# A GRU with an expert-choice layer behind it: state products by halves of the columns, VectorE's order in a step, and the order of the loads at the start

## The chip, the core and the metric

The kernel runs on one core of a Trainium2 chip. The metric is the time of one execution on the device in microseconds (us), of which the median of several runs is given. Beside the runs there is one profiled execution, from which all views of the trace come. TensorE is the matmul engine; each of its matmuls is preceded by a load of its stationary operand, shown as PEld. VectorE (DVE) and ScalarE (ACT) do the elementwise work, GpSimd (POOL) small copies, and SyncE (SP) issues most transfers.

## The reference

The input x has 16 sequences of 256 steps with 512 features. A GRU runs over the steps; its state h is 16 x 512, from `cond` at the start.

```python
gi = x @ W_ih + b_ih            # 512 -> 3 x 512
gh = h @ W_hh + b_hh
r = sigmoid(i_r + h_r)
z = sigmoid(i_z + h_z)
n = tanh(i_n + r * h_n)
h = (1 - z) * n + z * h
```

All 256 states form a 4096 x 512 matrix `xf`. A router computes `softmax(xf @ router_w + router_b)` over 16 experts; each expert takes its 256 tokens of highest weight. All experts share one matrix, so the output is x plus, for each token, the sum of the weights with which it was taken, times `xf @ expert_w + expert_b`. Everything is float32.

## The kernel before

**Layout.** A state product has only 16 rows. It is therefore laid out by four column tiles of the array: of the 512 columns of a gate, tile j computes every fourth group of 32, and its 128 columns land in partitions 32j and following of a PSUM bank (`quadrant`, `columns`). The contraction over 512 features is in four parts k. So one gate of one step is 4 k x 4 j = 16 matmul calls of 128 columns. In float32 each call becomes two loads and two matmuls in the trace. Two steps, an even and an odd one, form a pair p and share a bank half; the odd step multiplies both steps' states (32 columns of the stationary operand) so that its result lands beside the even one's.

**A step** (the loop over `s`). TensorE computes r and n over k = 0, 1, then r and n over k = 2, 3, then all of z (`h_part`, L424). The preset of these banks, by ScalarE copies, already holds x's contribution for r and z (from `ring`) and the bias for n (`preset_first` L384, `preset_rest` L387 and L394). ScalarE applies the sigmoid to r (L503). VectorE copies one element of r into `seen` (L507), multiplies r with h's part of n (L551), adds x's part (L553), each by halves of the columns. ScalarE applies tanh to the two halves (L555) and one sigmoid to all of z (L556). VectorE transposes both by 32 x 32 blocks (`turn_n` L563, `turn_z` L566), and computes u = h - n (L569), v = u z (L574) and the new state v + n (L577), each half by itself. The first half of the new state holds k = 0, 1, the second k = 2, 3.

While this chain runs, TensorE does other work in the same step: half of x's product for a pair six pairs ahead (`x_part` L401; `x_done` L412 adds the bias and stores it in `ring`), and, from the 13th step on, units of the expert product of finished groups (`expert` L368, one unit is a quarter of the columns for one k, four calls). Eight steps form a group g; a group's x is transposed into `xT` (two buffers, `turn_x` L234). The last expert products run after the steps (`late_part` L114), together with the search for each expert's threshold.

**The order** of all engines' work around the change is written out by hand (`manual_schedule`): each engine executes its instructions in the order of the program text, and semaphores are set between them where they touch the same data.

**The head**, before the first step. Six banks are zeroed and two spare banks zeroed repeatedly, each by four matmuls with a zero operand of 32 columns (`begin_sums`, `keep_clock`, L89). The input weights `wih` come gate by gate, each in two halves on SyncE's and ScalarE's queues, first r, then n, then z, with x's first group (SyncE) and `cond` (ScalarE) behind the first gate; `whh` follows by gates. x's second group comes on GpSimd's queue. TensorE transposes x's first group (`spread_x` L454, with VectorE copies L457), computes gate after gate for the first four pairs (`x_gate`), transposes `cond` and x's second group in between, adds the biases (`biases` L272), and completes the fifth pair. The sixth pair's product (index `AHEAD - 1` = 5) is spread over the odd steps of the first eight and stored at step 7.

Of the kernel before, what the change touches and what calls it, by code (L numbers as in the profile page):

```python
# [17 lines left out]
def kernel(  # L18
# [43 lines left out]
    zero = const.tile([P, QD], BF16, name="zero")  # L62
    nc.gpsimd.memset(zero, 0.0)
    make_identity(nc, ident)

# [19 lines left out]
    def begin_sums(bank):  # L85

        n = bank.shape[-1]
        for j in range(KC):
            nc.tensor.matmul(  # L89
                bank[QD * j : QD * (j + 1)],  # L90
                zero,
                zero[:, 0:E].unsqueeze(1).to_broadcast([P, n // E, E]),
                start=True,
                stop=True,
                tile_position=(0, QD * j),
            )

    early_groups = list(range(15))

# [64 lines left out]
    with (  # L164
# [78 lines left out]
        with tc.manual_schedule(engines={ET.SP, ET.Activation, ET.Pool}):  # L243
            def load_gate(dst, src, form, i, gate):
                load_rows(dst[:, :, i, :], src[:, gate * D : (gate + 1) * D], form)

            load_gate(wih, w_ih, "(p c) n -> p c n", 0, 0)
            nc.sync.dma_start(out=xs[:, 0, :], in_=x[:, 0:TG, :])
            nc.scalar.dma_start(out=c0, in_=cond)
            load_gate(wih, w_ih, "(p c) n -> p c n", 1, 2)  # L250
            load_gate(wih, w_ih, "(p c) n -> p c n", 2, 1)
            for gate in (0, 2, 1):
                load_gate(whh, w_hh, "(c p) n -> p c n", gate, gate)
            nc.scalar.activation(dummy, ones[0:1, 0:1], AF.Sigmoid)
            for dst, src in (
                (b_raw[0:1], b_ih.rearrange("(o g d) -> o g d", o=1, d=D)),
                (b_raw[1:2], b_hh.rearrange("(o g d) -> o g d", o=1, d=D)),
                (b_n, b_hh[2 * D :].rearrange("(o d) -> o d", o=1)),
            ):
                nc.gpsimd.dma_start(out=dst, in_=src)  # L260
            nc.gpsimd.dma_start(out=xs[:, 1, :], in_=x[:, TG : 2 * TG, :])
            for j in range(KC):
                load_xa(2, xa2, j, (nc.sync, nc.sync))
            nc.sync.dma_start(out=ewr[:, :, E:], in_=expert_w.rearrange("(c p) n -> p c n", c=KC))
            nc.sync.dma_start(out=ewr[:, :, 0:E], in_=router_w.rearrange("(c p) n -> p c n", c=KC))
            nc.gpsimd.dma_start(out=rb, in_=router_b.rearrange("(o e) -> o e", o=1).to_broadcast([P, E]))
            nc.sync.dma_start(out=eb, in_=expert_b.rearrange("(o d) -> o d", o=1).to_broadcast([P, D]))

        def biases(bank):
            for i, rows in enumerate((b_raw[:, 0, :], b_raw[0:1, 2, :], b_raw[:, 1, :], b_n)):  # L270
# [115 lines left out]
        def preset_rest(p):  # L386
            nc.scalar.copy(hn[p % 2], bias[:, 3, :])  # L387

            if p % (KC * TG // 2) == TG + 1:
                nc.scalar.copy(  # L390
                    lgt.rearrange("p (c e) -> p c e", e=QD),
                    zero.unsqueeze(1).to_broadcast([P, KC, QD]),
                )
            nc.scalar.copy(zz[p % 2], ring[:, p % AHEAD, 2, :])  # L394

        def x_part(p, k, bank, gates=slice(0, 3), start=True):
            g, pair = divmod(p, TG // 2)
# [15 lines left out]
                ring[:, p % AHEAD, :, :], bank[:, 0 : 3 * P].rearrange("p (g d) -> p g d", d=P), bias[:, 0:3, :], ALU.add  # L413
            )

        def h_part(s, gate, ks):
            p, odd = divmod(s, 2)
            m = QD if odd else B
            dst, gate_ = {"r": (rr[p % 2], 0), "z": (zz[p % 2], 1), "n": (hn[p % 2], 2)}[gate]
            for k in ks:  # L420

                lhs = hs[:, k, slot(s) - odd : slot(s) + 1, :].rearrange("p t b -> p (t b)")
                for j in range(KC):
                    nc.tensor.matmul(  # L424
                        dst[quadrant(j, m)],
                        lhs,
                        columns(whh[:, k, gate_, :], j),
                        start=False,
                        stop=(k == KC - 1),
                        tile_position=(0, QD * j),  # L430
                        skip_group_check=True,
                    )
# [8 lines left out]
        with tc.manual_schedule(engines={ET.PE, ET.Activation, ET.DVE}):  # L441
            for bank in banks:
                begin_sums(bank)
            keep_clock(8)
            held = (r_bank, n_bank, z_bank, x_bank0, x_bank1)

            def x_gate(p, gate):
                for k in range(KC):
                    x_part(p, k, held[p], slice(gate, gate + 1), start=False)
# [12 lines left out]
            keep_clock(2, (idles[1],))  # L462
            for p in range(KC):
                x_gate(p, 0)
            for p in range(KC):
                x_gate(p, 1)
            for k in range(KC):
                nc.tensor.transpose(idles[1][:, B * k : B * (k + 1)], c0[:, P * k : P * (k + 1)], ident[0:B, 0:B])
            nc.vector.tensor_copy(hs[:, :, 0, :], idles[1][:, 0 : KC * B].rearrange("p (k b) -> p k b", b=B))
            spread_x(1, idles[0])  # L470
            biases(l_bank)
            nc.vector.tensor_copy(bias, l_bank.rearrange("p (g d) -> p g d", d=P))
            for p in range(KC):
                x_gate(p, 2)
                x_done(p, held[p])
                if p == 0:
                    preset_first(0)
                elif p == 2:
                    preset_rest(0)
            for gate in range(3):  # L480
                x_gate(KC, gate)
            x_done(KC, held[KC])
            keep_clock(2)
        make_masks()
# [4 lines left out]
        with tc.manual_schedule(engines={ET.PE, ET.Activation, ET.DVE, ET.Pool, ET.SP}):  # L489
# [4 lines left out]
            for s in range(T):  # L494
                p, odd = divmod(s, 2)
                g, c = divmod(s, TG)
                for ks in (first, second):
                    h_part(s, "r", ks)
                    h_part(s, "n", ks)
                h_part(s, "z", range(KC))  # L500

                r = gp.tile([P, P], F32, name=f"r{odd}")
                nc.scalar.activation(r, rr[p % 2], AF.Sigmoid)  # L503
                if not odd and p < T // 2 - 1:
                    preset_first(p + 1)

                nc.vector.tensor_copy(seen[0:1, s % 8 : s % 8 + 1], r[0:1, 0:1])  # L507

                x_for = p + AHEAD if p + AHEAD < T // 2 else None
                x_bank = (x_bank0, x_bank1)[p % 2]  # L510
                if x_for:
                    for k in second if odd else first:
                        x_part(x_for, k, x_bank)
                if odd and s < TG:
                    x_part(AHEAD - 1, s // 2, idles[0], start=False)
# [33 lines left out]
                zs = gp.tile([P, P], F32, name=f"zs{odd}")  # L549
                for half, cols, ks in halves:  # L550
                    nc.vector.tensor_tensor(t[half], r[:, cols], hn[p % 2][:, cols], ALU.mult)  # L551
                for half, cols, ks in halves:
                    nc.vector.tensor_tensor(t[half], t[half], ring[:, p % AHEAD, 1, cols], ALU.add)  # L553
                for half, cols, ks in halves:
                    nc.scalar.activation(t[half], t[half], AF.Tanh)  # L555
                nc.scalar.activation(zs, zz[p % 2], AF.Sigmoid)  # L556
                if not odd and p < T // 2 - 1:
                    preset_rest(p + 1)
                if g and c < KC:
# [3 lines left out]
                    nc.vector.transpose(nT[half], t[half])  # L563

                def turn_z(half):
                    nc.vector.transpose(zT[half], zs[:, halves[half][1]])  # L566

                def less_n(half):
                    nc.vector.tensor_tensor(  # L569
# [9 lines left out]
                    )  # L579

                for f, half in (
                    (turn_n, 0), (turn_n, 1), (less_n, 0), (turn_z, 0), (less_n, 1),
                    (by_z, 0), (plus_n, 0), (turn_z, 1), (by_z, 1), (plus_n, 1),
                ):
                    f(half)

                if odd and x_for:
                    x_done(x_for, x_bank)
                if s == TG - 1:
                    x_done(AHEAD - 1, idles[0])  # L590
                if apart and odd:
                    less_max(g // KC - 1, lgt)
# [292 lines left out]
```

## Time and profile before

| | us |
|---|---|
| median of 3 runs | 1176.64 (1174.61 to 1176.87) |
| the profiled execution | 1177.37 |
| its span, from the first to the last instruction | 1175.6 |
| granted TensorE clock over the span | 0.997 of full speed |
| first state matmul of step 0 | 29.50 |
| end of the steps, about | 1102 |
| TensorE busy with matmuls | 1150.6 (98%) |
| weight loads | 940.5 (80%) |
| VectorE, ScalarE, GpSimd busy | 768.6, 387.0, 43.2 |

A line of the timeline gives the start in us from the span's start, the duration in us, the engine with the line of the kernel, the operation, output<-input by the program's names, shapes and a count; in brackets the engine's idle time before it and what released it. "issue" means that the engine waited for nothing that the profile shows. Neighbouring instructions of one kind are merged into one row. Matmuls overlap each other, so the time of one (273 ns at 128 columns) is not its price; the price is the distance from start to start. A row of windows gives the bounds, the length, then for PE, PEld, DVE, ACT and POOL the busy time and the number of instructions, then TensorE's granted clock, the transfers' share of the 16 DMA engines and GB/s. A row of the DMA queues gives queue, kind, packets, megabytes and share.

### The profile page before, as it was taken

How to read it: one execution, taken by the hardware profiler on the slowest of the kernel's cores; microseconds unless marked ns; L12 is line 12 of the kernel's file. 1: busy time of each engine (PE TensorE's matmuls, PEld its weight loads, DVE VectorE, ACT ScalarE, POOL GpSimd, SP SyncE). 2: the span in 40 equal slices, each digit the busy share in tenths (PEclk: the TensorE clock that was granted, in tenths of full speed). 3: DMA queues.
4: the chain of work that ended last, by engine and by line, in shares of the span. 5: the costliest groups of instructions: out<-in, count | busy, mean ns of one | idle time of the engine just before them, and what ended most of it. 6: DMA issues, size and time to landing. Idle time of an engine off the chain costs nothing.

```text
span 1175.6 us, 72806 instructions
## 1 busy us (share of the span) xinstructions
PE 1150.6 (98%) x32651; PEld 940.5 (80%) x32651; DVE 768.6 (65%) x4229; ACT 387.0 (33%) x1590; POOL 43.2 (4%) x241
## 2 busy tenths in 40 slices
PE   7999999999999999999999999999999999998898
PEld 5768888888888888888887888888888888888772
DVE  2556666666676666666666666666666666665674
ACT  0233333333333333333333333333333333333320
POOL 1000000000000000000000000000000000000000
PEclk9999999999999999999999999999999999999999
DMA  8000000000000000000000000000000000000127
GB/s 281 22 13 13 20 18 20 22 19 20 20 19 21 21 15 22 22 19 20 20 19 20 18 19 22 19 20 22 19 20 20 18 10 13 4 4 4 48 66 227
DMA packets 44237, 37.07 MB, mean 32 GB/s; under 512 B 6960, under 2 KB 35392, under 8 KB 43920
## 3 DMA queue, kind: packets, MB, share of 16 engines
q1 hardware_dynamic: 42048, 28.89, 8.4%
q8 instruction: 258, 4.23, 1.5%
q10 hardware_dynamic: 1664, 3.18, 0.8%
q14 instruction: 59, 0.48, 0.1%
q0 software_dynamic: 208, 0.28, 0.1%
HBM read 23.94 MB, written 8.39 MB: 28 GB/s over the span
## 4 chain that ended last, share of the span: by engine, by line
PE 95%; DVE 2%; issue 1%; DMA 1%; ACT 1%; SPq 0%; DVEq 0%
PE gates L424 57%; PE gates L401 27%; PE pe L114 5%; PE pe L368 5%; PE gates L303 1%; DMA xs<-in_x_dram 1%; DVE zT L566 0%; DVE nT L563 0%; DVE t L551 0%; ACT t L555 0%; ACT r L503 0%; PE idle L401 0%; DVE hs L577 0%; DVE v L574 0%; DVE t L553 0%
## 5 line engine op out<-in xcount | busy, mean ns | idle before, releaser
L424 PE MATMUL gates<-whh,hs 128*16 128x128 f32 x24576 | 727.5, 273 | 9.5 <-DVE zT L566 7.8
L424 PEld LDWEIGHTS gates<-whh,hs 128*16 128x16 f32 x24576 | 674.4, 103 | 41.6 <-ACT ht L291 15.8
L401 PE MATMUL gates<-wih,xt 128*32 128x384 f32 (+1 forms) x4384 | 380.6, 463 | 2.2 <-issue 2.2
L503 ACT ACTIVATE r<-gates 128x128 f32<-128x128 f32 x256 | 71.1, 278 | 556.8 <-PE gates L424 556.7
L401 PEld LDWEIGHTS gates<-wih,xt 128*32 128x32 f32 x4384 | 155.9, 110 | 83.1 <-issue 77.5
L507 DVE COPY seen<-r 1x1 f32<-1x1 f32 x256 | 36.3, 142 | 270.4 <-ACT r L503 270.4
L555 ACT ACTIVATE t<-t 128x64 f32<-128x64 f32 x512 | 103.1, 248 | 139.8 <-DVE t L553 139.8
L563 DVE STREAM_TRANSPOSE nT<-t 128x64 f32<-128x64 f32 x512 | 100.3, 234 | 47.9 <-ACT t L555 47.9
L566 DVE STREAM_TRANSPOSE zT<-zs 128x64 f32<-128x64 f32 x512 | 122.5, 239 | 0.2 <-ACT zs L556 0.2
L368 PEld LDWEIGHTS pe<-ewr,ht 128*32 128x32 f32 x1920 | 70.6, 110 | 61.0 <-issue 57.7
L577 DVE TENSOR_TENSOR hs<-v,nT 128x32 f32<-128x32 f32 x512 | 98.4, 192 | 17.4
L574 DVE TENSOR_TENSOR v<-u,zT 128x32 f32<-128x32 f32 x512 | 98.6, 193 | 8.8
L368 PE MATMUL pe<-ewr,ht 128*32 128x128 f32 x1920 | 93.0, 273 | 0.5 <-issue 0.4
L553 DVE TENSOR_TENSOR t<-t,xs 128x64 f32<-128x64 f32 x512 | 90.6, 218 | 0.0
L551 DVE TENSOR_TENSOR t<-r,gates 128x64 f32<-128x64 f32 x512 | 90.2, 218 | 0.4 <-PE gates L424 0.4
L569 DVE TENSOR_TENSOR u<-hs,nT 128x32 f32<-128x32 f32 x512 | 78.1, 153 | 0.0
L412 DVE TENSOR_TENSOR xs<-gates,bias 128x384 f32<-128x384 f32 x127 | 69.9, 550 | 3.3 <-PE gates L401 3.3
L556 ACT ACTIVATE zs<-gates 128x128 f32<-128x128 f32 x256 | 71.1, 278 | 1.4 <-ACT t L555 0.3
L114 PE MATMUL pe<-ewr,ht 128*32 128x128 f32 (+2 forms) x1320 | 65.4, 348 | 0.1
L114 PEld LDWEIGHTS pe<-ewr,ht 128*32 128x32 f32 x1320 | 37.6, 111 | 21.1 <-issue 19.2
L291 ACT COPY ht<-hs 128x128 f32<-128x128 f32 (+1 forms) x128 | 52.3, 411 | 0.8 <-DVE hs L577 0.8
L234 DVE STREAM_TRANSPOSE xt<-xa 128x256 f32<-128x256 f32 x58 | 38.8, 668 | 11.0 <-issue 6.6
(107 smaller groups left out, 300.6 us busy)
## 6 DMA issues: line engine op xcount, KB each, us to landing
out_dram<-xs SPq DMA_DIRECT2D x31, 256.0 KB, 3.8
xa<-in_x_dram SPq DMA_DIRECT2D x232, 32.0 KB, 1.9
xs<-in_x_dram SPq DMA_DIRECT2D x100, 64.0 KB, 2.3
wih<-in_L_cond_W_ih_dram SPq DMA_DIRECT2D x3, 512.0 KB, 10.6
wih<-in_L_cond_W_ih_dram ACTq DMA_DIRECT2D x3, 512.0 KB, 9.7
xs<-in_x_dram SPq DMA_DIRECT2D x6, 256.0 KB, 4.3
whh<-in_L_cond_W_hh_dram SPq DMA_DIRECT2D x3, 512.0 KB, 13.5
whh<-in_L_cond_W_hh_dram ACTq DMA_DIRECT2D x3, 512.0 KB, 12.4
```

What stands on the lines that cost most here:

```text
L114: nc.tensor.matmul(pe[q, cols], ht[:, g, k, q], ewr[:, k, E:][:, cols], start=False, stop=(k == KC - 1), tile_position=(0, QD * j), skip_g ...
L368: nc.tensor.matmul(pes[g][quadrant(j), at : at + P], ht[:, g, k, quadrant(j)], ewr[:, k, E + P * quarter : E + P * (quarter + 1)], start=F ...
L401: nc.tensor.matmul(bank[quadrant(j), at], lhs, columns(wih[:, k, gates, :].rearrange("p g d -> p (g d)"), j), start=start and k == 0, stop ...
L424: nc.tensor.matmul(dst[quadrant(j, m)], lhs, columns(whh[:, k, gate_, :], j), start=False, stop=(k == KC - 1), tile_position=(0, QD * j), ...
L551: nc.vector.tensor_tensor(t[half], r[:, cols], hn[p % 2][:, cols], ALU.mult)
L553: nc.vector.tensor_tensor(t[half], t[half], ring[:, p % AHEAD, 1, cols], ALU.add)
L555: nc.scalar.activation(t[half], t[half], AF.Tanh)
L563: nc.vector.transpose(nT[half], t[half])
L566: nc.vector.transpose(zT[half], zs[:, halves[half][1]])
L569: nc.vector.tensor_tensor(u[half], hs[:, halves[half][2], slot(s), :], of_step(nT[half], odd), ALU.subtract)
L574: nc.vector.tensor_tensor(v[half], u[half], of_step(zT[half], odd), ALU.mult)
L577: nc.vector.tensor_tensor(hs[:, halves[half][2], slot(s + 1), :], v[half], of_step(nT[half], odd), ALU.add)
```

## The change

In the steps, n's second part (k = 2, 3) is computed for the first half of each column tile's 128 columns, then for the second half; z likewise, all four k for the first half and then for the second. z's sigmoid is two instructions, one behind each half of the tanh. `seen` copies an element of n's bank, not of r. VectorE's last ten operations stand in another order. The sixth pair's x product lies in steps 0 to 3, one k in each, and is stored at step 4.

In the head, x's first group is issued first, `wih` comes by quarters of its rows (one k, all three gates, by halves of the columns on two queues), x's second group on ScalarE's queue ahead of the last quarter. TensorE computes all gates of four pairs for each k as it comes, with the transposes of `cond` behind k = 1 and the biases behind k = 2; then x's second group, then the fifth pair. A bank is zeroed by one matmul over all 128 partitions; the zero operand lies in a free corner of `xs`. The gates stand as r, z, n in `ring` and `bias` (r, n, z before).

```diff
     def begin_sums(bank):
         n = bank.shape[-1]
-        for j in range(KC):
-            nc.tensor.matmul(
-                bank[QD * j : QD * (j + 1)],
-                zero,
-                zero[:, 0:E].unsqueeze(1).to_broadcast([P, n // E, E]),
-                start=True,
-                stop=True,
-                tile_position=(0, QD * j),
-            )
+        nc.tensor.matmul(
+            bank, zero, zero[:, 0:E].unsqueeze(1).to_broadcast([P, n // E, E]), start=True, stop=True
+        )
...
-            load_gate(wih, w_ih, "(p c) n -> p c n", 0, 0)
+            def load_k(k):
+                rows = w_ih.rearrange("(p c) n -> p c n", c=KC)
+                to = wih.rearrange("p c g d -> p c (g d)")
+                for h, queue in enumerate(queues):
+                    cols = slice(3 * HD * h, 3 * HD * (h + 1))
+                    queue.dma_start(out=to[:, k, cols], in_=rows[:, k, cols])
+
             nc.sync.dma_start(out=xs[:, 0, :], in_=x[:, 0:TG, :])
+            load_k(0)
             nc.scalar.dma_start(out=c0, in_=cond)
-            load_gate(wih, w_ih, "(p c) n -> p c n", 1, 2)
-            load_gate(wih, w_ih, "(p c) n -> p c n", 2, 1)
+            load_k(1)
+            load_k(2)
+            nc.scalar.dma_start(out=xs[:, 1, :], in_=x[:, TG : 2 * TG, :])
+            load_k(3)
...
-            nc.gpsimd.dma_start(out=xs[:, 1, :], in_=x[:, TG : 2 * TG, :])
...
-        def h_part(s, gate, ks):
+        def h_part(s, gate, ks, half=None):
             p, odd = divmod(s, 2)
             m = QD if odd else B
+            cs = slice(0, KC) if half is None else slice(KC // 2 * half, KC // 2 * (half + 1))
+            at = slice(QD * cs.start, QD * cs.stop)
...
-                        dst[quadrant(j, m)],
+                        dst[quadrant(j, m), at],
                         lhs,
-                        columns(whh[:, k, gate_, :], j),
+                        columns(whh[:, k, gate_, :], j)[:, cs],
...
-            for p in range(KC):
-                x_gate(p, 0)
-            for p in range(KC):
-                x_gate(p, 1)
-            for k in range(KC):
-                nc.tensor.transpose(idles[1][:, B * k : B * (k + 1)], c0[:, P * k : P * (k + 1)], ident[0:B, 0:B])
-            nc.vector.tensor_copy(hs[:, :, 0, :], idles[1][:, 0 : KC * B].rearrange("p (k b) -> p k b", b=B))
-            spread_x(1, idles[0])
-            biases(l_bank)
-            nc.vector.tensor_copy(bias, l_bank.rearrange("p (g d) -> p g d", d=P))
+            for k in range(KC):
+                for p in range(KC):
+                    x_part(p, k, held[p], start=False)
+                if k == 1:
...
+                elif k == 2:
+                    biases(l_bank)
+                    nc.vector.tensor_copy(bias, l_bank.rearrange("p (g d) -> p g d", d=P))
+            spread_x(1, idles[0])
             for p in range(KC):
-                x_gate(p, 2)
                 x_done(p, held[p])
...
-                for ks in (first, second):
-                    h_part(s, "r", ks)
-                    h_part(s, "n", ks)
-                h_part(s, "z", range(KC))
+                for gate, ks, half in (
+                    ("r", first, None), ("n", first, None), ("r", second, None), ("n", second, 0), ("n", second, 1),
+                    ("z", range(KC), 0), ("z", range(KC), 1),
+                ):
+                    h_part(s, gate, ks, half)
...
-                nc.vector.tensor_copy(seen[0:1, s % 8 : s % 8 + 1], r[0:1, 0:1])
+                nc.vector.tensor_copy(seen[0:1, s % 8 : s % 8 + 1], hn[p % 2][0:1, 0:1])
...
-                if odd and s < TG:
-                    x_part(AHEAD - 1, s // 2, idles[0], start=False)
+                if s < KC:
+                    x_part(AHEAD - 1, s, idles[0], start=False)
...
                 for half, cols, ks in halves:
                     nc.scalar.activation(t[half], t[half], AF.Tanh)
-                nc.scalar.activation(zs, zz[p % 2], AF.Sigmoid)
+                    nc.scalar.activation(zs[half], zz[p % 2][:, cols], AF.Sigmoid)
...
                 for f, half in (
-                    (turn_n, 0), (turn_n, 1), (less_n, 0), (turn_z, 0), (less_n, 1),
-                    (by_z, 0), (plus_n, 0), (turn_z, 1), (by_z, 1), (plus_n, 1),
+                    (turn_n, 0), (turn_z, 0), (less_n, 0), (turn_n, 1), (by_z, 0),
+                    (turn_z, 1), (plus_n, 0), (less_n, 1), (by_z, 1), (plus_n, 1),
                 ):
                     f(half)
...
-                if s == TG - 1:
+                if s == KC:
                     x_done(AHEAD - 1, idles[0])
```

More of the change, by code (lines that the diff above doesn't have):

```diff
@@ L61 @@
     ones_b = const.tile([P, B], F32, name="ones_b")
-    zero = const.tile([P, QD], BF16, name="zero")
+    zero = xs[:, NG - 1, D - P // 2 :].bitcast(BF16)
     nc.gpsimd.memset(zero, 0.0)
@@ L269, in biases @@
         def biases(bank):
-            for i, rows in enumerate((b_raw[:, 0, :], b_raw[0:1, 2, :], b_raw[:, 1, :], b_n)):
+            for i, rows in enumerate((b_raw[:, 0, :], b_raw[:, 1, :], b_raw[0:1, 2, :], b_n)):
                 for j in range(KC):
@@ L391, in preset_rest @@
                     lgt.rearrange("p (c e) -> p c e", e=QD),
-                    zero.unsqueeze(1).to_broadcast([P, KC, QD]),
+                    zero.rearrange("p (c e) -> p c e", c=KC),
                 )
-            nc.scalar.copy(zz[p % 2], ring[:, p % AHEAD, 2, :])
+            nc.scalar.copy(zz[p % 2], ring[:, p % AHEAD, 1, :])
         def x_part(p, k, bank, gates=slice(0, 3), start=True):
@@ L445 @@
             held = (r_bank, n_bank, z_bank, x_bank0, x_bank1)
-            def x_gate(p, gate):
-                for k in range(KC):
-                    x_part(p, k, held[p], slice(gate, gate + 1), start=False)
             def spread_x(g, bank):
@@ L462 @@
             keep_clock(2, (idles[1],))
-            for p in range(KC):
-                x_gate(p, 0)
-            for p in range(KC):
-                x_gate(p, 1)
-            for k in range(KC):
-                nc.tensor.transpose(idles[1][:, B * k : B * (k + 1)], c0[:, P * k : P * (k + 1)], ident[0:B, 0:B])
-            nc.vector.tensor_copy(hs[:, :, 0, :], idles[1][:, 0 : KC * B].rearrange("p (k b) -> p k b", b=B))
-            spread_x(1, idles[0])
-            biases(l_bank)
-            nc.vector.tensor_copy(bias, l_bank.rearrange("p (g d) -> p g d", d=P))
-            for p in range(KC):
-                x_gate(p, 2)
+            for k in range(KC):
+                for p in range(KC):
+                    x_part(p, k, held[p], start=False)
+                if k == 1:
+                    for c in range(KC):
+                        nc.tensor.transpose(
+                            idles[1][:, B * c : B * (c + 1)], c0[:, P * c : P * (c + 1)], ident[0:B, 0:B]
+                        )
+                    nc.vector.tensor_copy(
+                        hs[:, :, 0, :], idles[1][:, 0 : KC * B].rearrange("p (k b) -> p k b", b=B)
+                    )
+                elif k == 2:
+                    biases(l_bank)
+                    nc.vector.tensor_copy(bias, l_bank.rearrange("p (g d) -> p g d", d=P))
+            spread_x(1, idles[0])
+            for p in range(KC):
                 x_done(p, held[p])
@@ L479 @@
                     preset_rest(0)
-            for gate in range(3):
-                x_gate(KC, gate)
+            for k in range(KC):
+                x_part(KC, k, held[KC], start=False)
             x_done(KC, held[KC])
@@ L548 @@
                 )
-                zs = gp.tile([P, P], F32, name=f"zs{odd}")
+                zs = [gp.tile([P, P // 2], F32, name=f"zs{odd}{half}") for half in range(2)]
                 for half, cols, ks in halves:
@@ L552 @@
                 for half, cols, ks in halves:
-                    nc.vector.tensor_tensor(t[half], t[half], ring[:, p % AHEAD, 1, cols], ALU.add)
+                    nc.vector.tensor_tensor(t[half], t[half], ring[:, p % AHEAD, 2, cols], ALU.add)
                 for half, cols, ks in halves:
                     nc.scalar.activation(t[half], t[half], AF.Tanh)
-                nc.scalar.activation(zs, zz[p % 2], AF.Sigmoid)
+                    nc.scalar.activation(zs[half], zz[p % 2][:, cols], AF.Sigmoid)
                 if not odd and p < T // 2 - 1:
@@ L565, in turn_z @@
                 def turn_z(half):
-                    nc.vector.transpose(zT[half], zs[:, halves[half][1]])
+                    nc.vector.transpose(zT[half], zs[half])
                 def less_n(half):
```

## The prediction

> **What bounds the kernel now.** I read the page first, then the timeline of one step, then the places where TensorE stops.
>
> ```profile
> PE 1150.6 (98%) x32651; PEld 940.5 (80%) x32651; DVE 768.6 (65%) x4229; ACT 387.0 (33%) x1590; POOL 43.2 (4%) x241
> PE 95%; DVE 2%; issue 1%; DMA 1%; ACT 1%; SPq 0%; DVEq 0%
> q8 instruction: 258, 4.23, 1.5%
> ```
>
> The chain of waits is TensorE for 95%. The third row, of the DMA queues, matters more than its 1.5% suggests: 4.23 MB in 258 packets are 16 KB each, and 4.23 MB over 2 x 32651 matmuls and weight loads are 65 bytes each. So queue 8 brings TensorE its own program, about 256 instructions a packet.
>
> One step without an expert unit, from the timeline (start, duration, engine, line):
>
> ```profile
> 401.46 2.81 PE L424 MATMUL gates<-whh,hs 128*16 128x128 f32 x96
> 403.02 0.28 ACT L503 ACTIVATE r<-gates 128x128 f32<-128x128 f32 x1 [2.43 <-PE gates L424]
> 403.46 0.35 DVE L551 TENSOR_TENSOR t<-r,gates 128x64 f32<-128x64 f32 x2
> 404.08 1.49 PE L401 MATMUL gates<-wih,xt 128*32 128x384 f32 x16
> 404.33 0.28 ACT L556 ACTIVATE zs<-gates 128x128 f32<-128x128 f32 x1
> 404.66 0.24 DVE L566 STREAM_TRANSPOSE zT<-zs 128x64 f32<-128x64 f32 x1
> 405.16 0.19 DVE L577 TENSOR_TENSOR hs<-v,nT 128x32 f32<-128x32 f32 x1
> ```
>
> The 96 state matmuls cost 2.62 us start to start (401.46 to 404.08), 27.3 ns each, and 16 x matmuls 1.29 us: 3.91 us. The other chain, from the first state matmul through r, t, zs, zT to the first half of hs (end 405.35), and 0.15 us until TensorE starts, takes 4.03. An expert unit adds 8 x 27.3 = 0.22 us to TensorE, so a step with one is bound by TensorE at 4.13 and one without by the chain at 4.03 to 4.07.
>
> Where TensorE stops with the mark "issue", which names no other engine (weight loads, late in the steps):
>
> ```profile
> 1065.75 0.25 PEld L368 LDWEIGHTS pe<-ewr,ht 128*32 128x32 f32 x10 [0.37 <-issue]
> 1065.90 0.12 PEld L424 LDWEIGHTS gates<-whh,hs 128*16 128x16 f32 x2
> 1066.00 0.12 PEld L368 LDWEIGHTS pe<-ewr,ht 128*32 128x32 f32 x2
> 1066.01 2.60 PEld L424 LDWEIGHTS gates<-whh,hs 128*16 128x16 f32 x92
> 1068.52 0.12 PEld L368 LDWEIGHTS pe<-ewr,ht 128*32 128x32 f32 x2
> 1068.62 0.10 PEld L424 LDWEIGHTS gates<-whh,hs 128*16 128x16 f32 x2
> 1068.63 0.55 PEld L368 LDWEIGHTS pe<-ewr,ht 128*32 128x32 f32 x18
> 1069.87 0.69 PEld L368 LDWEIGHTS pe<-ewr,ht 128*32 128x32 f32 x26 [0.69 <-issue]
> ```
>
> Between the two stops lie 10+2+2+92+2+2+18 = 128 loads, with their matmuls exactly 256 instructions. In the head the same count appears in the windows between its stops (ending at 16.17, 22.36 and 31.73 us):
>
> ```profile
> 15.00:22.00 7.00, 4.83 (x128) 4.21 (x127) 1.11 (x5) 0.00 (x0) 0.18 (x1) 1.00 1.05 381
> 22.00:31.00 9.00, 7.63 (x255) 7.04 (x256) 3.48 (x6) 0.81 (x3) 0.00 (x0) 1.00 0.58 188
> ```
>
> 255 and 511 records; with a semaphore instruction in each, one and two blocks of 256. TensorE stops because its next block has not come. The packets, found by narrowing the DMA view, start at 19.99 and 23.40, at 29.41 and 32.93, and at 1063.42, 1067.01 and 1071.25; TensorE resumes 2.3 to 2.9 us after the packet it waited for has started (1069.87 against 1067.01), and the next packet starts 1.0 to 1.4 us after that. So one block is fetched ahead, not more, and back to back one block takes 3.41, 3.52, 3.59 and 4.24 us, mean 3.69. Today it hides: from 100 to 900 us there are 181 packets, one each 4.42 us.
>
> **The change, part by part.** *State products by halves.* n's second part goes from 16 to 32 matmuls, z from 32 to 64, each of 64 columns. Time on the array: 27.3 ns at 128 columns and 1290/16 = 80.6 at 384 give 0.208 ns a column and 0.6 fixed, so 14.0 at 64: 96 x 14.0 in place of 48 x 27.3 is +0.03 us a step. That extrapolates below 128 columns; the other end is that a half costs as much as a whole, +1.31 us. [...]
>
> ```profile
> 1102.36 0.31 PE L114 MATMUL pe<-ewr,ht 128*32 128x128 f32 x3
> 1102.39 0.23 PE L317 MATMUL gates<-hs,ewr 128*16 128x16 f32 x3
> ```
>
> Each L114 matmul lasts about 297 ns, so three starts lie within 15 ns: on different column tiles they don't keep 25 ns apart. The three of L317, all on one tile, take 0.23 where one takes 178: about 25 ns apart there. A tile gets a half every 56 ns, so I take +0.03, 8 us over 256 steps at most.
>
> *Instructions.* Each added matmul brings its weight load: +48 pairs, +96 instructions a step. A step has now 192 + 32 + 13 (0.83 expert units of 16) + 1 = 238; then 334, or 1.31 blocks. Against 3.69 us a block this is 4.82 us a step where the mean is 4.15 now. That is the sum that decides. [...] TensorE would work through 256 instructions in 256/334 x 4.13 = 3.2 us.
>
> *The chain.* seen now reads hn, so it runs before r is there and its 0.14 us leaves the way from r to t: t can start when half of n is there, 403.46 - 0.22 + 0.13 = 403.37 rather than 403.46, -0.09 us. z's first half is ready 0.42 us earlier than all of z (404.33); its sigmoid now stands between the two tanh, and zT of half 0 follows nT of half 0. Then VectorE's own row sets hs: nT 404.18, zT 404.35, u 404.51, nT 404.62, v 404.78, zT 404.89, hs 405.05, -0.11 against 405.16. The chain becomes 3.92, level with TensorE's 3.94. The tanh of half 1, and behind it nT and u, queue on ScalarE behind the sigmoid that waits for z's half 0; it comes when that tanh could start anyway (404.06), so nothing, and 0.1 to 0.2 us where TensorE is late in z. ScalarE gets one instruction more a step (0.24 us); it is busy 33% and the copies behind have a pair's time. If all of it lay on the path: 61 us.
>
> *Early x parts.* Pair 5 is now done in steps 0 to 3, not in odd steps to 7. Same matmuls, but the second is what VectorE waits for here:
>
> ```profile
> 66.21 0.63 DVE L234 STREAM_TRANSPOSE xt<-xa 128x256 f32<-128x256 f32 x1 [4.42 <-PE idle L401]
> 68.81 4.44 PE L424 MATMUL gates<-whh,hs 128*16 128x128 f32 x96 [2.71 <-DVE zT L566]
> ```
>
> The transpose overwrites the xT that pair 5 still reads. TensorE loses 2.7 us, then 1.6 at a lowered clock (window 62 to 75: 0.87): about -4.5 us.
>
> *Head.* x is issued first, w_ih arrives by quarters, all gates of four pairs are done per quarter; zeroing takes 1 wide matmul, not 4. About 760 instructions go, so the stops at 14.0 and 20.7 us fall away: block two ends at the first step. The same 3.7 MB have to come before the last quarter (some 13 us at the 283 to 381 GB/s of the windows); from then 2.6 us for it, 0.8 for transposes, 3.4 for copies and pair 4, on top of work already queued: first step at about 23.5 instead of 29.5. Moving x's second group to ScalarE's queue costs an issue of 0.5 us there, hidden before its 11.9 us wait. The bias rows in another order cost nothing; the zero tile's larger memset may cost 0.1 us.
>
> **The sum.** From 30 to 1103 us the windows count 61,600 TensorE instructions; with 256 x 96 they are 86,200, or 336.6 blocks. 336.6 x 3.69 = 1242 us. Head 23.5 and tail 72.6 as now (1103 to 1175.6): span 1338. The early-x and chain gains drop out of it, since TensorE waits for its program anyway. The profiled execution took 1177.37 for a span of 1175.6, so +1.8; the median is 0.7 below it: 1339 us, +13.8%.
>
> **Rivals.** *Hidden fetch, faster.* If blocks come in time, gains show: head -6, stall -4.5, about 55 steps without a unit -0.1 each, against +0.03 in the 190 with one: about 1165 us. It decides at one number: the refill time at which 23.5 + 72.6 + 336.6 L equals 1175.6, L = 3.21 us. For it: nobody waits for a block between 75 and 1055 us (TensorE busy 979.96 of 980). Against: no back-to-back pair was under 3.41. [...] *Only half of it.* Refills run at their best, 3.41: 1246 us. *The chain edit doesn't act*, because zs or seen waits elsewhere: same 1339.
>
> **How the numbers follow.** Fetch-bound 0.80, with 1246 (3.41) to 1420 (3.93) as its own likely range; floor per matmul 0.07; hidden 0.12; between, near no change, 0.01. Low 1230, high 1430 leave out the hidden case, and most of the floor. A change under 0.2% can't be told from none here: faster 0.12, same 0.01, slower 0.87.
>
> **What would show it.** Right: queue 8 with about 349 packets, 3.6 to 3.8 us apart through the steps; TensorE idle marked "issue", some 0.6 us a step; the step's 96 half-width matmuls at 14 ns where no stop falls among them; no 4.42 us wait before L234's third use; first state matmul near 23.5. Wrong: packets closer than 3.2 us without stops (hidden), or 25 ns spacing inside the halves (floor).

## The result, and the profile after

The changed kernel takes 1383.19 us (median of 4 runs, 1382.96 to 1385.06) against 1176.76 (1174.61 to 1178.2) before: 1.176 times as long, 95% interval 1.1739 to 1.178. The prediction was 1339 us in a range of 1230 to 1430. The profiled span is 1381.3 us at a granted clock of 0.997, the same clock as before, so the 206 us are not a matter of the clock.

From the page of the changed kernel: the engines, the row of queue 8, the chain of waits, and three groups of instructions (engine, operation, output<-input, count, then busy us and mean ns, then the idle time ahead and what ended it):

```profile
PE 1227.1 (89%) x44559; PEld 980.0 (71%) x44559; DVE 723.9 (52%) x4229; ACT 408.0 (30%) x1846; POOL 42.5 (3%) x240
...
q8 instruction: 351, 5.75, 1.7%
...
PE 88%; issue 10%; DVE 1%; ACT 0%; POOL 0%; ACTq 0%; DVEq 0%; POOLq 0%
...
L428 PE MATMUL gates<-whh,hs 128*16 128x128 f32 (+1 forms) x36864 | 799.9, 238 | 118.6 <-issue 112.0
...
L571 DVE STREAM_TRANSPOSE zT<-zs 128x64 f32<-128x64 f32 x512 | 122.6, 239 | 134.5 <-ACT zs L561 129.3
...
L561 ACT ACTIVATE zs<-gates 128x64 f32<-128x64 f32 x512 | 112.3, 219 | 140.0 <-PE gates L428 132.1
```

The kernel before has these two rows for the same groups (without L566, whose idle time is 0.2 us there):

```profile
L424 PE MATMUL gates<-whh,hs 128*16 128x128 f32 x24576 | 727.5, 273 | 9.5 <-DVE zT L566 7.8
...
L556 ACT ACTIVATE zs<-gates 128x128 f32<-128x128 f32 x256 | 71.1, 278 | 1.4 <-ACT t L555 0.3
```

Matmuls went from 32651 to 44559 and queue 8's packets from 258 to 351. "issue", 1% of the chain before, is 10% now: 112 us of it stand in front of the state products (L428) alone, where TensorE waits for no other engine. The last two rows of the changed kernel show where it is passed on: z's sigmoids wait 132 us for TensorE, and the transposes of z 129 us for the sigmoids.

Windows of the changed kernel (bounds, length, busy us and instructions of PE, PEld, DVE, ACT and POOL, clock, DMA share, GB/s):

```profile
75.00:1255.00 1180.00, 1053.22 (x39721) 858.29 (x39714) 622.37 (x3777) 360.78 (x1677) 37.36 (x211) 1.00 0.06 16
1255.00:1305.00 50.00, 38.73 (x1647) 35.42 (x1649) 21.41 (x140) 15.20 (x67) 0.00 (x0) 0.97 0.04 10
```

In the steps TensorE is busy for 1053 of 1180 us; before it was for 979.96 of 980. Here is one of the stops, in the timeline of the changed kernel:

```profile
500.75 0.24 DVE L568 STREAM_TRANSPOSE nT<-t 128x64 f32<-128x64 f32 x1 [0.18 <-ACT t L560]
501.08 0.65 PEld L428 LDWEIGHTS gates<-whh,hs 128*32 128x32 f32 x42 [1.21 <-issue]
501.08 0.81 PE L428 MATMUL gates<-whh,hs 128*32 128x64 f32 x42 [1.05 <-issue]
...
502.04 0.22 ACT L561 ACTIVATE zs<-gates 128x64 f32<-128x64 f32 x1 [1.32 <-PE gates L428]
...
502.30 0.24 DVE L571 STREAM_TRANSPOSE zT<-zs 128x64 f32<-128x64 f32 x1 [1.30 <-ACT zs L561]
...
502.92 0.15 DVE L582 TENSOR_TENSOR hs<-v,nT 128x32 f32<-128x32 f32 x1
...
503.22 2.84 PE L428 MATMUL gates<-whh,hs 128*16 128x128 f32 x143
...
505.89 1.51 PE L403 MATMUL gates<-wih,xt 128*32 128x384 f32 x15
```

TensorE stops for 1.21 us with 42 loads of z still to do. Each later row of the elementwise chain then waits for the one before it, and the next step starts at 503.22. In that step no stop falls among the state products: from 503.22 to x's product at 505.89 they take 2.67 us, 96 of them half as wide as before, against 2.62 before.

From the records of the traces I counted, for the kernels below, the instructions on TensorE, the mean distance between starts of successive steps (24 to 243), the mean distance of queue 8's packets, and, over some 234 of the 256 steps, the boundaries of 256 instructions and those of them at which TensorE's weight loads stood still for over 0.15 us. The last column is the sum of these stops; where exactly the stretch begins and the idle time counts moves it by a few per cent. This table is used below.

| kernel | loads and matmuls | mean step | packet every | stops | their sum |
|---|---|---|---|---|---|
| before | 65302 | 4.151 us | 4.42 us | 6 of 218 | 2 us |
| after | 89118 | 4.981 | 3.79 | 223 of 305 | 182 |
| after_whole | 64542 | 4.151 | 4.42 | 2 of 216 | 0 |
| after_n_halves | 72734 | 4.387 | 4.12 | 55 of 244 | 53 |
| after_z_halves | 80926 | 4.668 | 3.93 | 146 of 275 | 110 |
| before_x_thirds | 80918 | 4.497 | 3.79 | 186 of 277 | 83 |
| before_halves | 89878 | 5.127 | 3.89 | 242 of 308 | 217 |
| halves_old_chain | 89118 | 5.082 | 3.86 | 236 of 305 | 205 |

### The profile page after: what moved, and what is told of

Read it like the earlier page. It is cut to its first block, busy times and chain, and to the rows that moved or that the text cites. A ratio compares the mean times of both kernels' runs of the same rounds, so it can differ in the third digit from the quotient of the medians.

```text
span 1381.3 us, 97011 instructions
## 1 busy us (share of the span) xinstructions
PE 1227.1 (89%) x44559; PEld 980.0 (71%) x44559; DVE 723.9 (52%) x4229; ACT 408.0 (30%) x1846; POOL 42.5 (3%) x240
## 4 chain that ended last, share of the span: by engine, by line
PE 88%; issue 10%; DVE 1%; ACT 0%; POOL 0%; ACTq 0%; DVEq 0%; POOLq 0%
PE gates L428 53%; PE gates L403 25%; PE pe L108 5%; PE pe L370 4%; PE gates L305 1%; PE gates L88 0%; PE idle L88 0%; PE idle L403 0%; DVE zT L571 0%; PE bank L679 0%; ACT zs L561 0%; PE idle L454 0%; PE bank L706 0%; PE gates L274 0%; DVE u L574 0%
## 5 line engine op out<-in xcount | busy, mean ns | idle before, releaser
L428 PE MATMUL gates<-whh,hs 128*16 128x128 f32 (+1 forms) x36864 | 799.9, 238 | 118.6 <-issue 112.0
L428 PEld LDWEIGHTS gates<-whh,hs 128*16 128x16 f32 x36864 | 727.5, 103 | 186.7 <-issue 149.8
L403 PE MATMUL gates<-wih,xt 128*32 128x384 f32 x4064 | 411.2, 487 | 19.2 <-issue 18.7
L512 DVE COPY seen<-gates 1x1 f32<-1x1 f32 x256 | 37.5, 146 | 390.2 <-PE gates L428 390.2
L560 ACT ACTIVATE t<-t 128x64 f32<-128x64 f32 x512 | 129.1, 252 | 168.0 <-DVE t L558 167.9
L561 ACT ACTIVATE zs<-gates 128x64 f32<-128x64 f32 x512 | 112.3, 219 | 140.0 <-PE gates L428 132.1
L568 DVE STREAM_TRANSPOSE nT<-t 128x64 f32<-128x64 f32 x512 | 122.7, 240 | 48.0 <-ACT t L560 47.9
L370 PEld LDWEIGHTS pe<-ewr,ht 128*32 128x32 f32 x1920 | 82.6, 110 | 56.6 <-issue 34.4
L370 PE MATMUL pe<-ewr,ht 128*32 128x128 f32 x1920 | 109.2, 273 | 5.7 <-issue 5.5
L579 DVE TENSOR_TENSOR v<-u,zT 128x32 f32<-128x32 f32 x512 | 87.6, 171 | 8.9
L582 DVE TENSOR_TENSOR hs<-v,nT 128x32 f32<-128x32 f32 x512 | 87.6, 171 | 8.7
L108 PEld LDWEIGHTS pe<-ewr,ht 128*32 128x32 f32 x1320 | 38.2, 113 | 20.5 <-issue 18.5
```

The costliest lines, as they stand in the source:

```text
L108: nc.tensor.matmul(pe[q, cols], ht[:, g, k, q], ewr[:, k, E:][:, cols], start=False, stop=(k == KC - 1), tile_position=(0, QD * j), skip_g ...
L370: nc.tensor.matmul(pes[g][quadrant(j), at : at + P], ht[:, g, k, quadrant(j)], ewr[:, k, E + P * quarter : E + P * (quarter + 1)], start=F ...
L403: nc.tensor.matmul(bank[quadrant(j), at], lhs, columns(wih[:, k, gates, :].rearrange("p g d -> p (g d)"), j), start=start and k == 0, stop ...
L428: nc.tensor.matmul(dst[quadrant(j, m), at], lhs, columns(whh[:, k, gate_, :], j)[:, cs], start=False, stop=(k == KC - 1), tile_position=(0 ...
L561: nc.scalar.activation(zs[half], zz[p % 2][:, cols], AF.Sigmoid)
L579: nc.vector.tensor_tensor(v[half], u[half], of_step(zT[half], odd), ALU.mult)
```

## The experiments

### Does the loss come from the halves at all?

`after_whole` is the changed kernel with n's second part and z as whole products again.

```diff
-                    ("r", first, None), ("n", first, None), ("r", second, None), ("n", second, 0), ("n", second, 1),
-                    ("z", range(KC), 0), ("z", range(KC), 1),
+                    ("r", first, None), ("n", first, None), ("r", second, None), ("n", second, None),
+                    ("z", range(KC), None),
```

> The changed kernel with n's second part and z as whole products again (16 calls per gate), all else as changed: sigmoid of z by halves, seen from n's bank, VectorE's new order, the new head, the early x parts. Refill theory (TensorE waits for its program; 3.80 us per block of 256 instructions as measured in the changed kernel): a step is back at 238 instructions, a block lasts over 4.2 us and the refill hides; the head's 6 us and the stall's 4.5 us stay: about 1165 us, under the kernel before. Rival (the sigmoid by halves or VectorE's new order costs the time): stays near 1380.

Measured: 1168.5 us (0.9936 of before, 95% interval 0.9919 to 0.9952; the brackets behind later medians give the same two). Without the halves the rest of the change is a gain of 7 to 8 us. `before_halves` is the other way round, the kernel before with that loop over halves and `h_part`'s `half` alone:

```diff
-                for ks in (first, second):
-                    h_part(s, "r", ks)
-                    h_part(s, "n", ks)
-                h_part(s, "z", range(KC))
+                for gate, ks, half in (
+                    ("r", first, None), ("n", first, None), ("r", second, None), ("n", second, 0), ("n", second, 1),
+                    ("z", range(KC), 0), ("z", range(KC), 1),
+                ):
+                    h_part(s, gate, ks, half)
```

> The kernel before with nothing changed but the products by halves (n's second part and z). Refill theory: 336.6 blocks x 3.80 = 1279 us, + 29.5 for the old head and 75 behind the steps: about 1384, as slow as the whole change. Rival (the slowdown comes from the other edits): near 1177.

Measured: 1423.85 us (1.2088, 1.2048 to 1.2128), 40 above what was expected. So the halves are the whole loss, and they cost more without the rest of the change than with it: 247 us on the kernel before, 215 on `after_whole`. The prediction has no room for that; it comes back below.

### Instructions or narrow matmuls?

`before_x_thirds` leaves the state products alone and cuts each matmul of x's product (384 columns) in three of 128. These are no narrower than the state products were before, but a step gets 64 instructions more.

```diff
-                        x_part(x_for, k, x_bank)
+                        for gate in range(3):
+                            x_part(x_for, k, x_bank, slice(gate, gate + 1), start=gate == 0)
```

> The kernel before with x's products in the steps cut by gates: three calls of 128 columns where one has 384. No matmul is narrower than before's own 128, and the state products aren't touched; 64 instructions more in each of 244 steps. Refill theory: (61,600 + 15,600) / 256 = 301.6 blocks x 3.80 = 1146 us, + 29.5 and 75: about 1250. Rival (narrow matmuls are slow): 12 calls' fixed parts alone, 8 quads more of 2.4 ns each a step, about 5 us: 1182.

Measured: 1263.9 us (1.0741, 1.0721 to 1.0761). From its page and its timeline:

```profile
q8 instruction: 319, 5.23, 1.8%
...
L424 PE MATMUL gates<-whh,hs 128*16 128x128 f32 x24576 | 771.2, 273 | 27.5 <-issue 16.1
```

```profile
507.69 0.50 PE L401 MATMUL gates<-wih,xt 128*32 128x128 f32 x10
508.46 1.18 PE L401 MATMUL gates<-wih,xt 128*32 128x128 f32 x34 [0.27 <-issue]
```

No matmul of it is below 128 columns, and yet it loses 87 us, with 186 stops at boundaries of 256 instructions and packets 3.79 us apart. The price is one of instructions: a narrow matmul is not needed for it.

### Each half of the dose

`after_n_halves` keeps only n's second part by halves (32 instructions a step more than `after_whole`), `after_z_halves` only z (64 more). The full change has 96 more.

```diff
-                    ("z", range(KC), 0), ("z", range(KC), 1),
+                    ("z", range(KC), None),
```

> The changed kernel with only n's second part by halves, z whole: 270 instructions a step. Refill theory: 61,600 + 256 x 32 instructions in the steps are 272.6 blocks, x 3.80 = 1036 us, less than the steps need anyway (about 1060), so hidden: 1165 to 1175 us. Rival (each added matmul has a price of its own, a floor on TensorE): a third of the way from 1165 to 1383, about 1238.

```diff
-                    ("r", first, None), ("n", first, None), ("r", second, None), ("n", second, 0), ("n", second, 1),
+                    ("r", first, None), ("n", first, None), ("r", second, None), ("n", second, None),
```

> The changed kernel with only z by halves, n's second part whole: 302 instructions a step. Refill theory: 304.6 blocks x 3.80 = 1157 us, + 24 for the head and 75 behind the steps: about 1256. Rival (a price for each added matmul): two thirds of the way from 1165 to 1383, about 1310.

Measured: 1224.52 us (1.041, 1.0391 to 1.0428) and 1296.59 (1.1037, 1.1006 to 1.1067): 56, 128 and, for both, 215 us over `after_whole`. Both expectations of the refill theory were too low, by 50 and 40 us. A price for each added matmul (the rival: 1238 and 1310) comes closer to these two by size, but not in kind: fixed prices would add up, and 56 and 128 make 184, not 215. The page of `after_n_halves` puts its loss on "issue":

```profile
q8 instruction: 287, 4.70, 1.6%
...
PE 94%; issue 4%; DVE 1%; DMA 1%; ACT 0%; SPq 0%; DVEq 0%; ACTq 0%
...
L428 PE MATMUL gates<-whh,hs 128*16 128x128 f32 (+1 forms) x28672 | 742.6, 257 | 41.1 <-issue 35.7
```

53 of its 56 us are in 55 stops at boundaries, and 189 other boundaries pass without one. What failed is the way of my sum: it compared the average time of a block with the refill, and an average that is long enough hides blocks that are not. In `after_n_halves` a step's state products are 224 instructions in 80 x 27.3 + 32 x 14 ns = 2.63 us. A block that takes them with one expert unit (16 instructions, 0.22 us) and only 8 matmuls of x (0.65 us) lasts 3.5 us, below the refill, and so much of the surplus elsewhere is no help: every late packet is followed by a stop at the very next boundary (30 of 30, below), so one block is fetched ahead and not more.

The second part of the loss is a refill that starts late. In the changed kernel half of the packets start 1.10 to 1.24 us after TensorE's first weight load behind a boundary. In `after_n_halves` 30 of 244 packets start over 1.9 us after it. Each of the 30 is followed by a stop at the next boundary, and these 30 stops are 39.8 of the 53 us; the other 214 packets leave 25 stops of 13.2 us together. In the changed kernel it is 30 of 305, with 43.3 of 182 us; in the kernel before none of 218 in the same stretch. The changed kernel shows how a late packet looks, in TensorE's weight loads and in the view of the DMA queues of 0.1 us:

```profile
496.23 0.09 PEld L428 LDWEIGHTS gates<-whh,hs 128*16 128x16 f32 x1 [1.16 <-issue]
...
497.70 1.90 PEld L428 LDWEIGHTS gates<-whh,hs 128*32 128x32 f32 x82
```

```profile
q8 instruction: 1, 0.02, 56.0%
```

A new block begins at 496.23, near the end of a step's program. At 497.70 the next step's first state load follows, which waits for the new state (written until 497.59, L582), and only in 498.6 to 498.7 does the packet for the following block start. The place decides. Of the 288 boundaries in steps 24 to 243 of the changed kernel, 25 have the next step's first state load 50 to 79 instructions behind them: all 25 packets are late. Of 9 at 40 to 49 instructions 4 are late; of the 37 nearer and the 217 farther none is. A late packet starts 0.9 to 1.4 us after that load. What holds the packet up there is not shown: no run takes that load's wait away. In the kernel before, 36 boundaries lie at the same 40 to 79 instructions, and their packets start 0.7 to 1.7 us ahead of the step's first state load: half of all its packets start within 0.46 us of their boundary (changed kernel: 1.15).

### Is it the distance of instructions or their number?

`after_x_quarter` is the changed kernel without three quarters of x's product in the steps, so that the same state products meet less other work.

```diff
-                    for k in second if odd else first:
+                    for k in range(0 if odd else 1):
```

> The changed kernel with three quarters of x's product in the steps left out (only k = 0, in the even steps, from pair 6 on; the gates are computed without the rest): 24 instructions and 0.97 us of matmul time less a step. Refill theory: (86,200 - 5,900) / 256 = 313.8 blocks x 3.80 = 1192 us, + 24 and 77: about 1293, although TensorE's own work and the chain would allow 3.95 us a step. Rival (the step is as long as its matmuls and its chain): 24 + 256 x 3.95 + 77, about 1112.

Measured: 1347.63 us (1.1455, 1.1434 to 1.1475). 12 of 16 x matmuls a step are gone, 0.97 us of TensorE's time (248 us over 256 steps) but only 24 of 334 instructions, and only 36 us come back. The row of queue 8 on its page, and its window over the steps:

```profile
q8 instruction: 328, 5.37, 1.6%
```

```profile
75.00:1230.00 1155.00, 865.09 (x37112) 746.68 (x37104) 623.95 (x3796) 361.43 (x1685) 37.21 (x210) 0.98 0.06 16
```

TensorE is busy for 865 of 1155 us and the kernel is still 171 us slower than before. That rules out the array's own work as the bound. The granted clock is 0.978 here (0.997 in the changed kernel); 2% of 865 us are 17, too little for the stops. The time is 54 us above the refill's sum: 52 of its 282 packets start late by the measure above, which is more than in any other kernel here, and 49 of those lead to a stop, 70.6 us in all. The late packets begin at 20 instructions between boundary and the step's wait, not at 40.

### Are the gains of the chain lost or not?

The prediction let the gains of the elementwise chain count nothing, since TensorE waits for its program anyway. Three runs bear on it. `halves_old_chain` is the changed kernel with the old chain:

```diff
-                nc.vector.tensor_copy(seen[0:1, s % 8 : s % 8 + 1], hn[p % 2][0:1, 0:1])
+                nc.vector.tensor_copy(seen[0:1, s % 8 : s % 8 + 1], r[0:1, 0:1])
...
-                zs = [gp.tile([P, P // 2], F32, name=f"zs{odd}{half}") for half in range(2)]
+                zs = gp.tile([P, P], F32, name=f"zs{odd}")
...
-                    nc.scalar.activation(zs[half], zz[p % 2][:, cols], AF.Sigmoid)
+                nc.scalar.activation(zs, zz[p % 2], AF.Sigmoid)
...
-                    nc.vector.transpose(zT[half], zs[half])
+                    nc.vector.transpose(zT[half], zs[:, halves[half][1]])
...
-                    (turn_n, 0), (turn_z, 0), (less_n, 0), (turn_n, 1), (by_z, 0),
-                    (turn_z, 1), (plus_n, 0), (less_n, 1), (by_z, 1), (plus_n, 1),
+                    (turn_n, 0), (turn_n, 1), (less_n, 0), (turn_z, 0), (less_n, 1),
+                    (by_z, 0), (plus_n, 0), (turn_z, 1), (by_z, 1), (plus_n, 1),
```

> The changed kernel with the old chain of the elementwise engines (one sigmoid over all of z, seen from r, VectorE's old order), the products still by halves. Theory of the prediction (TensorE waits for its program anyway, so the chain's gains drop out): the changed kernel's time within 5 us, 1378 to 1388 us. Rival (a stop in z holds the whole chain, so what lies behind z adds to the stop): the kernel before with halves alone took 1424 against 1383; the head and the early x parts are about 11 us of these 41, so 1383 + 30 = 1413 us, and a mean step of about 5.1 us in place of 4.98.

`halves_one_sigmoid` has only the three edits of `zs` among these, and keeps the new `seen` and the new order.

> The changed kernel with one sigmoid over all of z behind both tanh, the rest of the changed chain and the halves kept. If the chain matters through z's first half alone (ready before a stop that falls in the second), this is nearly all of the old chain's loss: 1405 to 1415 us, perhaps more, since VectorE's new order asks for zT before it has turned n's second half. If the order or seen carries it: 1383 to 1390. If the chain's gains drop out: 1378 to 1388.

Measured: 1402.7 us (1.1904, 1.1883 to 1.1926) and 1406.13 (1.1938, 1.1909 to 1.1967). The old chain costs 19.5 us where the halves are in, and the single sigmoid alone costs as much. So the gain is not lost, against the prediction, and it needs z's sigmoid by halves: `seen` and the new order, which `halves_one_sigmoid` keeps, win nothing without it (the intervals of the two runs overlap). What they add beside it was not run. It is smaller than the 30 us that I had put down to the chain from `before_halves`. The program on TensorE has the same boundaries in both kernels, so steps can be compared one by one, sorted by the place in the step where a block ends (steps 16 to 239, mean us from step to step):

```
block ends in                        steps   after   old chain   sum of the differences
r or n                                 71    4.287     4.316          2.0 us
r or n, and a second time in x etc.    44    5.093     5.200          4.8
z's first half                         56    5.142     5.256          6.4
z's second half                        27    5.351     5.495          3.9
r or n, and z's second half            26    5.943     6.079          3.6
```

13.9 of the 20.6 us are in the 109 steps with a block's end in z, 0.11 to 0.14 us each. With a stop in z the whole way through sigmoid, transposes and the update stands behind TensorE, and what is shorter there is saved. Where the stop falls in r or n, with the chain behind it hidden again by x's product, 0.03 us is left. The second row doesn't fit this account: it gains 0.11 us a step, 4.8 us in all, though no block ends in z there, and why is open. The first row shows the other thing that matters: a step whose block ends in r or n takes 4.29 us, and with a stop in z 5.1 to 5.4.

`whole_old_chain` asks the same where nothing stops: `after_whole` with the edits of the last diff.

> The kernel with whole products and the new head and early x parts (after_whole, 1168.5 us), with the chain put back: one sigmoid for z behind both tanh, seen from r, VectorE's old order. If the chain's edits bring the 0.1 us in the 55 steps without an expert unit that I worked out: 5 us slower, about 1174. If the steps are bound by TensorE and by the refill's phase there too: unchanged, 1168 to 1169.

Measured: 1165.2 us (0.9908, 0.9893 to 0.9923). The old chain isn't slower here; if anything it is 3 us faster, though the two intervals overlap a little. The mean step is 4.150 us against 4.151, so the new chain gave nothing in the steady steps. The 3.1 us between the two spans lie in the last 15 steps (65.4 and 69.0 us); the head differs by 1 us the other way. In `after_whole` a block comes late inside z there, and behind it TensorE runs at a lowered clock:

```profile
1063.49 0.41 PE L428 MATMUL gates<-whh,hs 128*32 128x128 f32 x3 [0.83 <-issue]
...
1065.17 4.41 PE L428 MATMUL gates<-whh,hs 128*16 128x128 f32 x96 [1.27 <-DVE u L574]
```

96 state matmuls take 4.41 us there where 2.8 is usual, at a granted clock of 0.66 in the window from 1065 to 1070. Whether the chain's order brings that stop about or only the place where a block happens to end, I did not test.

### The early x product

`before_early_x` is the kernel before with pair 5's product in steps 0 to 3 alone.

```diff
-                if odd and s < TG:
-                    x_part(AHEAD - 1, s // 2, idles[0], start=False)
+                if s < KC:
+                    x_part(AHEAD - 1, s, idles[0], start=False)
...
-                if s == TG - 1:
+                if s == KC:
```

> The kernel before with nothing changed but the sixth pair's x product, moved into steps 0 to 3 and stored at step 4. My account of the stall at 65.6 us: VectorE's transpose no longer waits for step 7's product, TensorE doesn't stop and its clock doesn't fall: -4.5 us, about 1172. Rival (the stop only moves, or has another cause): 1176.8, unchanged.

Measured: 1172.41 us (0.9967, 0.9955 to 0.9979), some 4 us gained, as expected; in the traces the first 12 steps take 53.0 us in place of 57.2. In its timeline the transpose that waited 4.42 us for TensorE now waits for nothing, and the state products of the step run at 2.83 us:

```profile
62.19 2.83 PE L424 MATMUL gates<-whh,hs 128*32 128x128 f32 x96
...
62.86 0.67 DVE L234 STREAM_TRANSPOSE xt<-xa 128x256 f32<-128x256 f32 x1 [0.21 <-issue]
```

## Why the prediction was right, and where it was off

**What decides: right.** The step that decided was "336.6 x 3.69 = 1242 us". 351 packets came where 349 were named, and in the steps they are 3.79 us apart. The sum let TensorE wait at every boundary; at 82 of 305 it did not, but the packets there follow each other no more slowly (3.56 us on average in steps 24 to 243), so little is lost by it. `before_x_thirds` shows the same limit with whole-width matmuls, and `after_x_quarter` with less work on the array. In the kernel before the same refill was hidden, with 2 us of stops at 218 boundaries; in the changed one it was not, with 182 us at 305.

**The size: 44 us too low, in the refill term.** 336.6 blocks at 3.79 instead of 3.69 us are 34 of them. The packets of the steps fall in two sorts: 90% at a mean of 3.66 us, just below the 3.69 taken from four gaps, and 10% at about 5.07, where the packet starts late. The prediction had measured back-to-back refills and had no term for a packet that starts late; 0.1 x (5.07 - 3.66) is 0.14 us a block. Of the other 10 us, 0.4 are the head (first state matmul at 23.89 for 23.5) and some 2 the end (79.4 us from the start of the last step, 77.5 before). Most of the rest is in the last 15 steps, which take 81.0 us where 15 mean steps are 74.7; the clock was 0.97 there, and the cause is open. Part of the closeness is luck: with the old chain the same products take 1402.7 us, 64 above the prediction, and only the chain's gain, which the sum left out, brings this down to 44.

**Halves at 14 ns: right.** 2.67 us for the 144 state matmuls of an undisturbed step, 2.65 by the prediction's durations. Starts 25 ns apart, as the kernel before has them between L317's matmuls on one tile, would have made it 48 x 27.3 + 96 x 25 = 3.71 us. The halves, which go round the four column tiles, come out at (2.67 - 48 x 0.0273) / 96 = 14.2 ns.

**"The early-x and chain gains drop out of it": wrong.** This is the step that failed. With the halves in, `halves_old_chain` loses 19.5 us to the changed kernel. Waiting for a block and the chain don't lie side by side, as a maximum of two would have it; a stop in z puts the chain behind it and the two add, which the sorted steps show for 13.9 of 20.6 us. The pieces of the 44 us between the profiles of `before_halves` and the changed kernel: the chain 21 (spans 1402.7 and 1381.3), and of the 23 that are left, the head 6 (first state matmul at 30.9 and 24.8 us, `halves_old_chain`), the first eight steps with the early x product 5, the end some 3, and some 9 over the steady steps, which no edit of mine explains; the blocks end at other places in those two programs.

**The chain's own -0.1 us in 55 steps: not there.** It was named for the rival of the hidden fetch. `whole_old_chain` has the same mean step without it. That a step without a unit was bound by the chain by 0.1 us was read from starts and ends in one step, a margin too thin for that.

**Head and early x: right in sum.** `whole_old_chain` gains about 11 us over before; 4.4 of it is the early x product by its own run, which leaves about 7, where the prediction had 6 for the head. The changed kernel's first state matmul is at 23.89 us (23.5 by the prediction, 29.50 before), but in `after_whole` it is at 25.05 and in `whole_old_chain` at 26.07. There the head itself brings 3.4 us; the first 12 steps are 6.4 us shorter, 2.2 more than by the early x product alone, and the end 1.3. The stall is gone in the changed kernel too:

```profile
60.49 0.67 DVE L228 STREAM_TRANSPOSE xt<-xa 128x256 f32<-128x256 f32 x1 [0.21 <-issue]
```

**The rivals.** *Hidden fetch* would have given 1165 us. That is what the same edits give without the halves, 1165.2 and 1168.5; so its sum was good and its premise wrong: it decides from 3.21 us a block on, and the packets of the changed kernel are 3.79 apart, the shortest distance 3.27. *The chain edit doesn't act* is excluded by `halves_old_chain`. *Only half of it* took 3.41 us a block; the shortest sort had a mean of 3.66. *The floor per matmul*, 0.07 in the chances: no run shows a floor of 25 ns across column tiles. The undisturbed step showed 14.2 ns a half, and `after_x_quarter` gave back 36 us where 248 us of TensorE's time had gone.

## What to carry to other kernels

Count TensorE's instructions as well as its time: here a block of 256, that is 128 matmuls with their loads, took about 3.7 us to bring in, with one block fetched ahead, and cutting matmuls in two for an earlier result cost time in every run here (56 to 247 us); what has to last longer than the refill is each single block, not the average one. Where a step does stop for its program, the place of the stop decides what else counts, and a chain that is hidden otherwise can come onto the path behind it (0.11 to 0.14 us of the chain's gain showed in a step with a block's end in z, 0.03 in one whose only block's end is in r or n). Head and early x product without the halves and with the old chain (`whole_old_chain`) are the fastest version measured: 1165.2 us, 0.9908 of before, with `after_whole` 3 us behind and overlapping intervals.

## What the runs showed that I had not expected

The refill of TensorE's program can start late (over 1.9 us after the boundary), and where the step's wait stands in the block decides it: with the wait 50 to 79 instructions behind the boundary all 25 packets of the changed kernel were late, and every late packet was followed by a stop. Why is not shown. The kernel before has the same wait at the same distances and no late packet: its packets there start 0.7 to 1.7 us ahead of the step's first state load; why half of them start within 0.46 us of their boundary, against 1.15 in the changed kernel, is open.

The costs of added instructions do not simply add up (56, 128 and 215 us for 32 in n, 64 in z, and both). 64 in the wide products of x cost 87 us, 64 in z 128; since these two kernels differ in their elementwise order and head too, that the place makes this difference is not shown.
